# Where the halves of a modulation sum stand among the evictions of the block ahead of it

## Chip, cores and metric

The kernel runs on one core of one Trainium2 chip. A core has TensorE (PE, matmuls; its weight loads are shown as PEld), VectorE (DVE), ScalarE (ACT), GpSimd (POOL) and SyncE (SP, whose queue issues nearly all DMAs here). Each engine works off its own queue in order, and the engines meet at semaphores. The metric is the device time in microseconds, as the median of several runs.

## What is computed

The reference, cut to what matters (x is 64 x 64 x 512, cond is 64 x 256; all in fp32):

```python
q = relu(cond @ W3 + b3)                                  # 64 x 512
v = (64 * x + x.sum(axis=1, keepdims=True)) * q[:, None]  # the modulation
y = relu(v @ W2 + b2)
base   = y @ W_base + b_base
shared = (y @ A_s) @ B_s
gates  = softmax(y @ W_router + b_router)                 # 6 experts, the best 2 kept
routed = sum over e of ((y @ A_r[e]) * w[e]) @ B_r[e]
out = x + base + shared + routed
```

The sum over axis 1 is the modulation sum: for each of the 64 batches and each feature, a sum over 64 tokens.

## The kernel before

The 4096 tokens are worked on in four blocks k of 1024 tokens (16 batches). Features lie on the partitions in four chunks of 128, which are taken in the order `CHUNKS = (0, 2, 1, 3)`. A block has two stages.

The **first stage** makes y = relu(v @ W2 + b2). Block 0 has its own form, `first_mixed`, in which the first half of its tokens is computed directly, and the second half with sums of rows and of weights (a Strassen-like scheme with seven products; the products are made by `product`, L170). Blocks 1 to 3 use `first_inner`, the same scheme nested twice (L446).

Behind it PE computes **ph** (L779), the product of y with the low-rank matrices and the router. DVE makes the row sums **sy** of y (L263 to L266), and the **second stage**, `second`, begins: `gate` (L578 to L604, on DVE, with one exponential on ACT), then the products with W_base (L170, banks named ox, oy, oz, ow), copies on ACT that seed one bank from another (L629), the transposes of the gated low-rank values hw (L704), and the routed products (L641).

While a block is in these stages, the kernel prepares the *next* block. `prepare(k)` builds the list `behind` for block k. An entry of this list is a few steps, and `fill(n)`, called at fixed places between the current block's work, takes the next n entries off and issues them. The order is written out by hand: an engine's queue holds exactly what the calls issue, in their order. The steps are:

- `sums(c, half)` (L206 to L208, DVE): for chunk c and one half of the 16 batches, the reduction over the tokens (L207) and its product with q (L208); half 0 also makes 64 q (`nq`, L206) for all 16.
- `batch(c, b)` (L212, ACT): modulates one batch of one chunk in place, with `nq` as scale and the sum as bias.
- steps of weight sums (`also`, L137 to L140 and L161 to L164), and of row sums (L263 to L266, L315 to L318), on DVE.

The pairs are 32 entries with two batches each, eight for each chunk. Sums are put into chosen pairs, ahead of the batches: those of the second chunk (chunk 2) into pairs 4 and 5, those of the later ones into pairs 16, 19 and 20. Each of the first four `also` steps (L137 to L140) stands at the end of one of the first four pairs. Before all pairs stands one entry with both halves of the sum of the first chunk.

In `first_mixed` the calls are one `fill(1)` directly behind `prepare(1, ...)`, and then, for each of two rounds j:

```python
            product(py, 6, j, t2, s, start=j == 0)
            nc.vector.tensor_tensor(u, py, p1[:, j], ALU.add)        # L408
            product(pw, 5, j, t2, s, start=j == 0)
            nc.vector.tensor_tensor(r, pw, u, ALU.add)               # L410
            product(pz, 7, j, t2, s, start=j == 0)
            nc.vector.tensor_tensor(r, pz, r, ALU.add)               # L412
            relu(y, f2, 1, r, other)
            fill(1)
            product(pw, 3, j, t2, s, start=False)                    # r2: L416
            ...
            fill(1)
            product(pz, 4, j, t2, s, start=False)                    # r1: L420
            ...
            fill(1)
```

The second product into pw adds to the bank that L410 reads, so it waits for L410. Behind the second round follow ph on PE, sy on DVE, a fill of 8 entries (in block 0) or 4 (later blocks), and `second`.

Of the kernel before, what the change touches and what calls it, by code (L numbers as in the profile page):

```python
# [36 lines left out]
def adaln_ffn(ctx: ExitStack, tc: tile.TileContext, xa, x0, x1, head, w3, w2, wb, a, bcat, br, outT):  # L37
# [25 lines left out]
    def load_x(k):  # L63
        xs[k] = xpool.tile([P, NC, 2, TB], F32, tag="x", name=f"x_{k}")
        for c in CHUNKS:
            nc.sync.dma_start(xs[k][:, c].rearrange("p h t -> p (h t)"), x1[k, c])
# [126 lines left out]
    def modulate(k):  # L193


        vs[k] = v = xs[k]
        vsum = small.tile([P, NC, BB], F32, tag="vsum", name=f"vsum_{k}")
        nq = small.tile([P, NC, BB], F32, tag="nq", name=f"nq_{k}")

        def sums(c, half):  # L200

            bs = ts(half, BB // 2)
            xc = v[:, c].rearrange("p h (b n) -> p b h n", n=NH)[:, bs]
            q = q_sb[:, c, ts(k, BB)]
            if half == 0:
                nc.vector.tensor_scalar(nq[:, c], q, float(N), None, ALU.mult)  # L206
            nc.vector.tensor_reduce(vsum[:, c, bs], xc, AX.XY, ALU.add)  # L207
            nc.vector.tensor_tensor(vsum[:, c, bs], vsum[:, c, bs], q[:, bs], ALU.mult)  # L208

        def batch(c, b):  # L210
            x = v[:, c, :, ts(b, NH)]
            nc.scalar.activation(x, x, AF.Identity, bias=vsum[:, c, b : b + 1], scale=nq[:, c, b : b + 1])  # L212

        return ({c: [lambda c=c, n=n: sums(c, n) for n in range(2)] for c in CHUNKS},
                {c: [lambda c=c, b=b: batch(c, b) for b in range(BB)] for c in CHUNKS})
# [39 lines left out]
    def row_sums(a, name, cols=slice(0, TB)):  # L255

        all_s = mid.tile([P, 4, KH, TB], F32, tag=name, name=name)
        s = [all_s[:, i, :, cols] for i in range(4)]
        a11, a12, a21, a22 = a[:, :KH, 0, cols], a[:, KH:, 0, cols], a[:, :KH, 1, cols], a[:, KH:, 1, cols]

        def steps(c=slice(0, KH)):
            return [
                lambda: nc.vector.tensor_tensor(s[0][:, c], a21[:, c], a22[:, c], ALU.add),  # L263
                lambda: nc.vector.tensor_tensor(s[1][:, c], s[0][:, c], a11[:, c], ALU.subtract),
                lambda: nc.vector.tensor_tensor(s[2][:, c], a11[:, c], a21[:, c], ALU.subtract),
                lambda: nc.vector.tensor_tensor(s[3][:, c], a12[:, c], s[1][:, c], ALU.subtract),  # L266
            ]

        return {1: a11, 2: a12, 3: s[3], 4: a22, 5: s[0], 6: s[1], 7: s[2], "sums": all_s}, steps

    behind = []

    def fill(n):
        for _ in range(min(n, len(behind))):
            for step in behind.pop(0):
                step()

    def prepare(k, also=()):

        if k == NB:
            return
        sums, batches = modulate(k)
        ss[k], row_steps = row_sums(vs[k], "s")
        early, late = row_steps(slice(0, 1)), row_steps(slice(1, 2))
        c0, c1, c2, c3 = CHUNKS
        pairs = [batches[c][b : b + 2] for c in CHUNKS for b in range(0, BB, 2)]
        for places, steps in (((4, 5), sums[c1]), ((16, 16), sums[c2]), ((19, 20), sums[c3]),
                              ((25, 27, 29, 31), early)):  # L290
            for n, step in zip(places, steps):
                pairs[n].insert(0, step)
        for n, step in enumerate(also):
            pairs[n if n < 4 else 12 + n].append(step)
        behind.append(sums[c0])
        behind.extend(pairs)
        behind.extend([step] for step in late + prepare_inner(k))

# [43 lines left out]
    def first_mixed(y):  # L342
# [51 lines left out]
        for step in t2_steps + inner_steps[:4] + s_steps():  # L394
            step()
        prepare(1, tb_steps + inner_steps[4:])
        fill(1)
        pairs = temps(0)
# [25 lines left out]
    def first_inner(k, y):  # L424


        order = (1, 5, 6, 7, 2, 3, 4)
        prepare(k + 1)
        t_side, s_side = inner_t, inner[k]["s"]
        inner[k]["places"]()  # L430
# [87 lines left out]
        q(2, 1)  # L518
        for step in inner[k]["late"]:
            step()  # L520
        fill(1)
        for t in range(2, 7):
            open_banks(t)
            take_1(t - 2)
# [81 lines left out]
    def load_rows(k):  # L606

        res = {}
        for n, (f, h) in zip(pair_tags[2:3] + pair_tags[:2] + pair_tags[3:], ((1, 0), (1, 1), (0, 0), (0, 1))):
            res[f, h] = tmp.tile([P, KH, TB], F32, tag=n, name=f"x{n}_{k}")  # L610
            nc.sync.dma_start(
                res[f, h], x1[k, f * KH : (f + 1) * KH, :, ts(h, TB)].rearrange("c p t -> p c t")
            )
        return res
# [143 lines left out]
    for k in range(NB):  # L758
        y = mid.tile([P, NC, 2, TB], F32, tag="y", name=f"y_{k}")
        rest = None  # L760
        if k == 0:
            first_mixed(y)
        else:
            rest = first_inner(k, y)
        res = load_rows(k)
        if k == 0:
            load_x(3)

        ph = ps_h.tile([P, 2 * NS, P], F32, tag="ph", name=f"ph_{k}")
        groups = [(h, s) for h in range(2) for s in range(NS)]
        if not rest:
            groups.sort(key=lambda g: g[1] // KH)
        for n, (h, s) in enumerate(groups):
            if rest and n == 2:
                rest()
            for c in range(NC):
                nc.tensor.matmul(  # L779
                    ph[:, h * NS + s, :HC], y[:, c, h, ts(s, P)], a_sb[:, c, :],  # L780
                    start=(c == 0), stop=(c == NC - 1),
                )
        sys_[k], steps = row_sums(y, "sy")
        for step in steps():
            step()
        fill(4 if k else 8)
        second(k, y, ph, res)


# [48 lines left out]
```

## Time and profile before

| | us |
|---|---|
| median of 3 runs | 262.75 (262.47 to 262.76) |
| the profiled execution | 262.98 |
| its span | 261.2 |
| PE busy | 255.4 (98% of the span) |
| DVE busy | 193.9 (74%) |
| ACT busy | 136.6 (52%) |
| POOL busy | 38.7 (15%) |
| share of the chain that ended last: PE, DVE, ACT, DMA | 87%, 7%, 2%, 2% |

Block 0's stages lie in the span as follows: `first_mixed` to 35.2 us, ph from 35.2 to 42.5, the second stage to 74.2, where block 1's first product starts. Two stretches of it, from the table of windows (the columns are the length, then the busy time and number of instructions of PE, PEld, DVE, ACT and POOL, the granted clock of PE, the DMA share and GB/s):

```profile
27.24:29.08 1.84, 1.02 (x5) 0.57 (x4) 1.65 (x5) 0.00 (x0) 0.00 (x0) 1.00 0.95 376
29.08:35.23 6.15, 6.15 (x29) 5.42 (x30) 5.28 (x13) 4.42 (x12) 0.00 (x0) 1.00 0.30 119
```

In the first of them PE is busy for 1.02 of 1.84 us; in the second, all the time. A line of the timeline is: start, length, engine, line, operation, output and inputs with their shapes, number of instructions merged, and in brackets how long the engine had idled before it and what ended that. Matmuls of a timeline overlap, so that the start of a group is a better mark than its end.

### The profile page before, as it was taken

What the parts mean: (1) busy time and instruction counts of PE and PEld (TensorE: products, weight loads), DVE (VectorE), ACT (ScalarE), POOL (GpSimd) and SP (SyncE); (2) the same over time, 40 slices, a digit from 0 to 9 for tenths busy, and PEclk for the clock granted to TensorE, in tenths of its full rate; (3) what the DMA queues carried; (4) which work ended last, traced back from release to release, by engine and by line L of the source; (5) the groups of instructions that cost most, each with busy time, mean ns of one, the idle gap of its engine ahead of it and who ended that gap; (6) DMA issues with size and microseconds to landing.
All of it is one profiled execution on the core that took longest, in us unless ns stands there. A gap on an engine that the chain in (4) does not pass through costs nothing.

```text
span 261.2 us, 3176 instructions
## 1 busy us (share of the span) xinstructions
PE 255.4 (98%) x1004; PEld 164.6 (63%) x1004; DVE 193.9 (74%) x386; ACT 136.6 (52%) x373; POOL 38.7 (15%) x53
## 2 busy tenths in 40 slices
PE   7999899999999999999999999999999999999995
PEld 3755797454468889445458889644447889745452
DVE  2899987879968976967995894987895476872332
ACT  2299586588037897279106889349504428112000
POOL 1000000001008420002005640001000770000100
PEclk9999999999999999999999999999999999999999
DMA  7997719503320045000431025200332022400133
GB/s 167 382 337 285 282 32 375 235 3 111 130 80 0 4 148 174 0 3 0 164 117 41 0 80 160 86 0 3 120 120 80 0 74 92 160 0 3 72 141 109
DMA packets 14145, 28.54 MB, mean 109 GB/s; under 512 B 1472, under 2 KB 2496, under 8 KB 14128
## 3 DMA queue, kind: packets, MB, share of 16 engines
q1 hardware_dynamic: 13840, 28.21, 30.8%
q8 instruction: 8, 0.13, 0.2%
q10 hardware_dynamic: 288, 0.13, 0.2%
q14 instruction: 9, 0.07, 0.1%
HBM read 19.94 MB, written 8.39 MB: 108 GB/s over the span
## 4 chain that ended last, share of the span: by engine, by line
PE 87%; DVE 7%; ACT 2%; DMA 2%; issue 0%; SPq 0%; DVEq 0%
PE ia L446 13%; PE ph L779 11%; PE oz L170 11%; PE ox L170 11%; PE ib L446 10%; PE ow L170 9%; PE oy L170 5%; PE ow L641 5%; PE ox L641 3%; PE oz L641 3%; DMA w_sb<-in_w_dram 2%; DVE vsum L228 1%; PE pt L704 1%; PE last L650 1%; ACT y L340 1%; PE yw L170 1%
## 5 line engine op out<-in xcount | busy, mean ns | idle before, releaser
L212 ACT ACTIVATE x<-x,vsum,nq 128x64 f32<-128x64 f32 x192 | 67.6, 431 | 7.0 <-DVE vsum L208 7.0
L779 PE MATMUL ph<-a_sb,y 128*128 128x118 f32 x256 | 30.5, 276 | 0.3 <-ACT y L340 0.3
L779 PEld LDWEIGHTS ph<-a_sb,y 128*128 128x128 f32 x256 | 30.0, 192 | 1.2 <-ACT y L340 0.7
L437 DVE TENSOR_TENSOR u<-ib,u 128x256 f32<-128x256 f32 x42 | 16.4, 418 | 18.5 <-PE ib L446 18.3
L452 ACT COPY ib<-ia 128x256 f32<-128x256 f32 x21 | 7.6, 360 | 42.3 <-PE ia L446 42.3
L170 PE MATMUL ox<-y,wb_sb 128*128 128x512 f32 x64 | 29.5, 593 | 0.0
L708 POOL TENSOR_TENSOR hwd<-hwT 112x512 f32<-112x512 f32 x4 | 5.8, 1451 | 137.6 <-ACT hwT L706 137.6
L170 PEld LDWEIGHTS ox<-y,wb_sb 128*128 128x128 f32 x64 | 11.9, 190 | 13.4 <-issue 13.2
L437 DVE TENSOR_TENSOR u<-ia,u 128x256 f32<-128x256 f32 (+1 forms) x36 | 16.1, 461 | 2.9 <-ACT u L484 1.6
L340 ACT ACTIVATE y<-u,head_sb 128x256 f32<-128x256 f32 (+1 forms) x30 | 15.8, 584 | 4.0 <-DVE u L412 4.0
L446 PE MATMUL ib<-inner_s,inner_t 128*128 128x256 f32 x60 | 17.8, 384 | 0.0
L637 DVE SCALAR_TENSOR_TENSOR xu<-oz,head_sb,xu 128x512 f32<-128x512 f32 x16 | 12.0, 749 | 7.2 <-PE oz L170 4.8
L207 DVE TENSOR_REDUCE vsum<-x 128x8 f32<-128x512 f32 x24 | 16.2, 675 | 0.0
L170 PE MATMUL oz<-sy,tb 128*128 128x512 f32 x32 | 15.2, 599 | 0.0
L170 PE MATMUL oz<-y,tb 128*128 128x512 f32 x32 | 15.1, 592 | 0.0
L170 PE MATMUL oy<-sy,tb 128*128 128x512 f32 x32 | 15.0, 592 | 0.0
L354 PE MATMUL py<-v,w_sb 128*128 128x512 f32 (+1 forms) x40 | 14.4, 510 | 0.6 <-DMA w_sb<-in_w_dram 0.6
L170 PE MATMUL ow<-sy,wb_sb 128*128 128x512 f32 x28 | 13.2, 592 | 0.0
L170 PE MATMUL ow<-sy,tb 128*128 128x512 f32 x28 | 13.2, 592 | 0.0
L455 ACT COPY ib<-ib 128x256 f32<-128x256 f32 x21 | 7.6, 363 | 9.9 <-PE ib L446 9.9
L446 PEld LDWEIGHTS ib<-inner_s,inner_t 128*128 128x128 f32 x60 | 11.2, 190 | 2.2 <-ACT ib L455 0.8
L250 ACT ACTIVATE v<-x,vsum,nq 128x64 f32<-128x64 f32 x32 | 11.0, 428 | 1.9 <-DVE vsum L248 1.9
(173 smaller groups left out, 462.2 us busy)
## 6 DMA issues: line engine op xcount, KB each, us to landing
xu<-in_x_dram SPq DMA_DIRECT2D x16, 512.0 KB, 4.2
out_dram<-xu SPq DMA_DIRECT2D x30, 256.0 KB, 2.0
x<-in_x_dram SPq DMA_DIRECT2D x12, 512.0 KB, 7.8
x<-in_x_dram SPq DMA_DIRECT2D x7, 256.0 KB, 5.7
w_sb<-in_w_dram SPq DMA_DIRECT2D x4, 256.0 KB, 5.7
wb_sb<-in_wb_dram SPq DMA_DIRECT2D x4, 256.0 KB, 5.1
w_sb<-in_w_dram SPq DMA_DIRECT2D x1, 384.0 KB, 5.5
out_dram<-xu SPq DMA_DIRECT2D x2, 192.0 KB, 1.9
```

The costliest lines, as they stand in the source:

```text
L170: nc.tensor.matmul(ps, w[i][:, c, ts(j, P)], s[i][:, c, :], start=start and c == 0, stop=c == KH - 1, skip_group_check=True,)
L207: nc.vector.tensor_reduce(vsum[:, c, bs], xc, AX.XY, ALU.add)
L212: nc.scalar.activation(x, x, AF.Identity, bias=vsum[:, c, b : b + 1], scale=nq[:, c, b : b + 1])
L250: nc.scalar.activation(v[:, c, :, ts(b, NH)], batches_of(c, b, b + 1)[:, :, 0], AF.Identity, bias=vsum[:, c, b : b + 1], scale=nq[:, c, b ...
L340: nc.scalar.activation(y[:, f, h, cols], src, AF.Relu, bias=b2_sb[:, f : f + 1])
L354: nc.tensor.matmul(p[:, :, lo * NH : hi * NH], w2_sb[:, c, ts(f, P)], v[:, c, :, lo * NH : hi * NH], start=(c == 0 and lo == 0), stop=(c = ...
L437: add = lambda o, a, b: nc.vector.tensor_tensor(o, a, b, ALU.add)
L446: nc.tensor.matmul(bank[b, t][:, cols], t_side(o, n), s_side(o, n), start=n == 1, stop=True, skip_group_check=True,)
L452: nc.scalar.copy(bank["b", t][:, lo], bank["a", t][:, lo])
L637: nc.vector.scalar_tensor_tensor(t, ps[name, j], bb_sb[:, f : f + 1], t, ALU.add, ALU.add)
L641: nc.tensor.matmul(ps[name, j], bcat_sb[:, ts(f, P)], hw, start=False, stop=True, skip_group_check=True)
L779: nc.tensor.matmul(ph[:, h * NS + s, :HC], y[:, c, h, ts(s, P)], a_sb[:, c, :], start=(c == 0), stop=(c == NC - 1),)
```

## The change

```diff
@@ prepare
-        for places, steps in (((4, 5), sums[c1]), ((16, 16), sums[c2]), ((19, 20), sums[c3]),
+        for places, steps in (((4, 4 if k == 1 else 5), sums[c1]), ((16, 16), sums[c2]), ((19, 20), sums[c3]),
                               ((25, 27, 29, 31), early)):
...
-        behind.append(sums[c0])
+        behind.extend([step] for step in sums[c0])
         behind.extend(pairs)
@@ first_inner
         for step in inner[k]["late"]:
             step()
-        fill(1)
+        fill(2)
@@ the loop over blocks
-        fill(4 if k else 8)
+        fill(4 if k else 9)
         second(k, y, ph, res)
```

The one entry with both halves of the first chunk's sum becomes two entries with one half each. In `first_mixed` the `fill(1)` behind `prepare(1, ...)` thus issues half 0 alone, half 1 comes with the first fill of the first round (behind L412), and each pair one fill later than before. In `first_inner` the first fill takes two entries in place of one, so that both halves still come together there. The fill ahead of block 0's second stage takes 9 entries in place of 8, so that the same entries are left for the second stage. For block 1's preparation (k == 1) both halves of chunk 2's sum now stand in pair 4 (half 1 first, since each is inserted at the front); pair 4 is what the last fill of the second round issues.

## The prediction

> **What bounds the kernel now.** I read the busy table first: TensorE (PE) is busy 98% of the 261.2 us span, and in the chain that ended last it holds 87%. So almost any saving must be a place where PE stands still. I therefore went to the list of waits and looked for PE as the waiting engine, then to the timeline of PE and VectorE (DVE) around the one entry that lies in the code that is changed. From the list of waits (engine, line, what was waited for: us in total, times, longest):
>
> ```profile
> PEld yw L170 <- DVE u L410: 1.2, 1, 1.2
> PE yw L170 <- DVE u L410: 0.8, 1, 0.8
> DVE lg L578 <- PE ph L779: 0.8, 1, 0.8
> ```
>
> PE waits once, in block 0, for the eviction at L410. The timeline of PE there (start, us, what):
>
> ```profile
> 26.37 1.03 PE L170 MATMUL yw<-s,t 128*128 128x256 f32 x4
> 27.24 1.03 PE L170 MATMUL yz<-s,t 128*128 128x256 f32 x4
> 29.08 1.13 PE L170 MATMUL yw<-s,w_sb 128*128 128x256 f32 x4 [0.82 <-DVE u L410]
> 30.05 1.03 PE L170 MATMUL yz<-v,t 128*128 128x256 f32 x4
> ```
>
> A group of four normally starts 0.86 us after the one before (26.37 to 27.24). Between yz and yw it is 1.84, so the stall is **0.98 us** from start to start. What DVE did meanwhile:
>
> ```profile
> 26.49 0.68 DVE L207 TENSOR_REDUCE vsum<-x 128x8 f32<-128x512 f32 x1
> 27.20 0.17 DVE L208 TENSOR_TENSOR vsum<-vsum,q_sb 128x8 f32<-128x8 f32 x1
> 27.28 0.68 DVE L207 TENSOR_REDUCE vsum<-x 128x8 f32<-128x512 f32 x1
> 27.99 0.17 DVE L208 TENSOR_TENSOR vsum<-vsum,q_sb 128x8 f32<-128x8 f32 x1
> 28.08 0.42 DVE L408 TENSOR_TENSOR u<-yy,p 128x256 f32<-128x256 f32 x1
> 28.60 0.42 DVE L410 TENSOR_TENSOR u<-yw,u 128x256 f32<-128x256 f32 x1
> 29.13 0.42 DVE L412 TENSOR_TENSOR u<-yz,u 128x256 f32<-128x256 f32 x1
> ```
>
> The two pairs L207/L208 are the two halves of the modulation sum of chunk 0 for the next block. Both stand ahead of L408 and L410, and L408's input yy had been ready for 1.5 us (yy ended at 26.53). The chain that ended last goes through exactly these rows: the DVE sums of s, the two halves, L408, L410, then yw, and from there PE nearly alone to the end.
>
> **What is removed from the path.** The second half (27.28 to 28.08, start to start **0.80 us**) now stands behind L412. L408 starts at 27.28. L410 waits for L408's result, and the two start 0.52 apart, so L410 runs from 27.80 to 28.22; its other input, yw, ended at 27.40. PE was released 0.06 after L410 ended (29.02 to 29.08), so yw starts at 28.28. Sum: 29.08 - 28.28 = **0.80 us** earlier. PE alone could have started at 28.10 (27.24 + 0.86), so 0.18 of the stall stays, and 0.98 is the most that this place can yield.
>
> One rule asks for a different size. The Trainium skill, "VectorE: DVE Perf Modes", section "The DRAIN you can't avoid", has each DVE operation followed by a flush of about its duration less 266 ns in which the next one doesn't start. Read as time behind the operation, a half would free 0.68 + 0.41 + 0.17 = 1.26 us, and PE's own pace would then cut the gain to 0.98. The rows say otherwise: L208 starts 0.71 behind an L207 of 0.68, and L408 starts 0.09 behind an L208 of 0.17. I take 0.80. The same skill's "TensorE: Matmul & The Clock Gate", first part, has PE's clock halved after an idle window of some 3.4 us; a stall of 0.98 is far under it, and the granted clock is 1.00 in the windows around it, so no clock bonus is added to the 0.80.
>
> **What is added behind L412.** L412 then runs at 28.33 (yz, which it needs, ends at 28.27), and its release of the next product yz is in time. The half follows and with it everything in DVE's queue: L416, L137, L420, L138, then the second round's L408, L410. Three things ask for these:
> - PE's second-round yw needs yw's bank read by L416. L416 starts at 29.64 (28.33 + 0.51 + 0.80) and ends at 30.06; the product starts at 31.77 - 0.80 = 30.97. Slack 0.9. Likewise L420, ending near 31.0, against 31.84. Both cost nothing.
> - The second L410 must let PE's second yw<-s,w_sb start, which stood at 33.50 and now wants 32.70. From L412 to the second L408 DVE took 2.99 (29.13 to 32.12). One fill step (L139, 0.60 start to start) drops behind, the half (0.80) comes in: 3.19. So L408 starts at 31.52, and L410 at 32.04, just when its product is done (32.80 - 0.80 = 32.00). It ends at 32.46, releases at 32.52, and 0.18 is left. **This is the thinnest cover of the change.** If DVE is later by more than 0.18, PE waits for the rest, one for one.
> - ScalarE's (ACT's) relu evictions wait for L416 and L420. ph (64 rows, started at 35.23) needs the columns that they write only behind its first 32 rows, 3.6 us after its start: before, the last of them ended at 36.81, against 38.8. Nothing.
>
> **What moves ahead of the gate.** The pairs of batches slip by one place. In the second round L139 and L140 fill the two gaps, and both halves of chunk 2's sum (0.80 each and an L206 of 0.08) come behind the last L420, which makes the last eviction earlier: L412 32.90, L139 33.24, L416 33.84, L140 34.18, L420 34.78 to 35.20, instead of an end at 36.27. The row sums sy begin 3.28 + 0.60 = 3.88 behind the second L412, at 36.78 (before: 36.98), and end 4.75 later, at 41.53. The gate's first row L578 waits for ph, whose end moves from 42.53 to 41.73. So the 0.84 of idle time of DVE there shrinks to about 0.2, but stays: the gate starts 0.80 earlier too. If that cover were gone, DVE would be late at the gate only; its result hw (47.89) is asked for by PE at 56.11, so nothing follows. ACT: the last eviction starts near 35.24; behind it 20 batches instead of 18, at 0.337 each (6.06/18), from 35.65 to 42.39, and the exponential wants ACT at 43.28 - 0.80 = 42.48. It fits, just. Its queue holds the seed copies next, and the first of them wants 43.55. SP: its four row loads wait for the last eviction and go out about 1.05 earlier, and the four loads of x behind them too; nothing waits on them before 48.33. POOL's queue is passed by nothing.
>
> **Behind the gate** the number of queued steps is the same as before, and so is each engine's order in blocks 1 to 3: there both halves still stand in one place, since two entries are taken where one was. Both queue ends behind the gate are released by PE: DVE idles 0.44 for ACT's copy of a PE result, ACT idles 11.02 before block 1. So the 0.80 is a plain shift of all that follows; the only non-PE pieces in the later chain (ACT evictions near 94 and 155, and a DVE row at 258) are themselves behind PE.
>
> **Sum.** The profiled execution took 262.98 (span 261.2, 1.78 around it): 262.98 - 0.80 = 262.18. It stood 0.23 above the median of the three runs, 262.75, so against that median: **261.95 us**. 0.2%, about what a measurement of this kernel can tell from no change, is 0.53 us; the three runs lie within 0.29.
>
> **Rivals.**
> - *The wait comes back in the second round.* For it: only 0.18 of cover at the second L410, and L137 carries two waits for transfers, which is where the 0.51 behind L412 came from. Against it: the weights were issued by 13.5 and landed within 5.6. If DVE is 0.55 late there, 0.37 is handed back: gain 0.43, **262.3**.
> - *The shift is swallowed later.* For it: block 1 has DVE finishing inner_s at 75.4 while PE is already in that block, so PE there is close to being DVE's. Against it: DVE's busy stretch before it is released by ACT batches that follow PE's transposes, so it shifts too. If two thirds go there: **262.5**.
> - *Slower: ACT's longer run of batches.* Twenty batches stand between the last eviction and the gate's exponential and seed copies. The copy of y is asked for by PE at 45.0, and can start at 43.55 and end at 44.12; ACT must be 1.7 us behind my sum before PE waits, and 2.5 before the gain is gone. If the batches took 0.49 each in place of 0.337 (20 x 0.15 = 3.0 us), the end is **263.2**. Batches of this kind ran at 0.337 in that very stretch, so I hold it unlikely.
> - *That the change doesn't do what it says* I see no room for: the order of DVE's instructions moves as told.
>
> **How the numbers follow.** 0.80 gained (between 0.65 and 0.98): 81%. Second round: 9%. Swallowed: 6%. Slower: 4%. The likeliest gives 261.95. Its gain bounds (0.98 and 0.65) give 261.77 and 262.10; with the spread of the runs (0.15 each way) 261.6 to 262.25, and up to 262.35 it takes in most of the second-round case. Faster by over 0.2% (under 262.22): nearly all of the first case and a fifth of the second, 80%. Within 0.2%: 16%. Slower: 4%.
>
> **What would show it.** PE's yw at about 28.3 with a wait of about 0.1; the second yw<-s,w_sb without one; ph at 34.4; L578 still waiting for ph, by 0.1 to 0.3; block 1's first ia near 73.4 instead of 74.17; granted clock 1.00. Wrong would be: PE waiting for DVE in front of the second yw, the first yw earlier by less than 0.7, or later blocks whose distance from ph has changed.

## Result

| | before | changed |
|---|---|---|
| median of 11 runs each, us | 262.65 | 261.70 (261.42 to 262.31) |
| ratio, 95% interval | | 0.9966 (0.9949 to 0.9982) |
| profiled execution, its span, us | 262.98, 261.2 | 261.56, 259.8 |

The kernel became faster by 0.95 us in these runs, 0.36%; 261.95 had been forecast. The whole interval lies under 1, and its upper end (0.18%) just within what was called no change.

PE's timeline of the changed kernel, over the same products as before:

```profile
24.77 1.10 PE L170 MATMUL yy<-s,t 128*128 128x256 f32 x4
25.71 1.03 PE L170 MATMUL yw<-s,t 128*128 128x256 f32 x4
26.58 1.03 PE L170 MATMUL yz<-s,t 128*128 128x256 f32 x4
27.63 1.13 PE L170 MATMUL yw<-s,w_sb 128*128 128x256 f32 x4
28.59 1.03 PE L170 MATMUL yz<-v,t 128*128 128x256 f32 x4
...
32.05 1.03 PE L170 MATMUL yw<-s,w_sb 128*128 128x256 f32 x4
32.91 1.03 PE L170 MATMUL yz<-v,t 128*128 128x256 f32 x4
33.77 7.30 PE L779 MATMUL ph<-a_sb,y 128*128 128x118 f32 x64
```

From yz to yw it is now 1.05 us instead of 1.84. No wait is noted in brackets, but 0.19 over the pace of 0.86 is left: yw starts 0.06 behind the end of L410, as before. The second round runs at 0.86 from group to group. DVE's timeline of the same kernel shows the half in its new place, and what is left of DVE's idle time ahead of the gate:

```profile
26.54 0.17 DVE L208 TENSOR_TENSOR vsum<-vsum,q_sb 128x8 f32<-128x8 f32 x1
26.62 0.42 DVE L408 TENSOR_TENSOR u<-yy,p 128x256 f32<-128x256 f32 x1
27.15 0.42 DVE L410 TENSOR_TENSOR u<-yw,u 128x256 f32<-128x256 f32 x1
27.68 0.43 DVE L412 TENSOR_TENSOR u<-yz,u 128x256 f32<-128x256 f32 x1
28.02 0.68 DVE L207 TENSOR_REDUCE vsum<-x 128x8 f32<-128x512 f32 x1
...
30.68 0.41 DVE L408 TENSOR_TENSOR u<-yy,p 128x256 f32<-128x256 f32 x1
31.39 0.42 DVE L410 TENSOR_TENSOR u<-yw,u 128x256 f32<-128x256 f32 x1 [0.29 <-PE yw L170]
...
41.11 0.21 DVE L578 TENSOR_TENSOR lg<-ph,br_sb 128x48 f32<-128x48 f32 x1 [0.23 <-PE ph L779]
```

The two profiled spans differ by 1.4 us, more than the medians. So the span has to be cut into pieces that can be compared: to the first yy, from there to the start of ph, to block 1's first ia, and to the end. Each start is read from PE's timeline.

| us | to first yy | yy to ph | ph to first ia | ia to the end |
|---|---|---|---|---|
| before | 25.43 | 9.80 | 38.94 | 187.0 |
| changed | 24.77 | 9.00 | 38.95 | 187.1 |

All that the change does is in the second piece: **0.80 us**. The first piece is 0.66 shorter here, but lies ahead of anything that was moved; the last section shows where its scatter comes from. The pieces behind ph are equal to 0.1 us, so nothing was handed back.

In the chain that ended last, the DVE work between yy and the second yw is gone; the chain now stays on PE there (the chain of the changed kernel in order of time; columns are start, length, what):

```profile
25.88 0.86 PE yw L170 x4
26.74 0.86 PE yz L170 x4
27.63 1.13 PE yw L170 x4
```

Ahead of yy the chain says less about the change. In the kernel before it went mainly over DVE from 9.84 on, in this profile of the changed kernel over PE; but in the first run below, which has the same split, it goes over DVE again, up to L264 at 24.76.

### The profile page after: what moved, and what is told of

The parts are those of the page before. It is cut to its first block, busy times and chain, and to the rows that moved or that the text cites. A ratio compares the mean times of both kernels' runs of the same rounds, so it can differ in the third digit from the quotient of the medians.

```text
span 259.8 us, 3177 instructions
## 1 busy us (share of the span) xinstructions
PE 254.8 (98%) x1004; PEld 164.5 (63%) x1004; DVE 193.9 (75%) x386; ACT 136.5 (53%) x373; POOL 38.7 (15%) x53
## 4 chain that ended last, share of the span: by engine, by line
PE 94%; ACT 2%; DMA 2%; SPq 0%; issue 0%; DVE 0%
PE ia L446 13%; PE ph L779 11%; PE oz L170 11%; PE ox L170 11%; PE ib L446 10%; PE ow L170 9%; PE py L354 5%; PE oy L170 5%; PE ow L641 5%; PE oz L641 3%; PE ox L641 3%; DMA w_sb<-in_w_dram 2%; PE yw L170 1%; PE pt L704 1%; PE last L650 1%; PE yz L170 1%
## 5 line engine op out<-in xcount | busy, mean ns | idle before, releaser
L207 DVE TENSOR_REDUCE vsum<-x 128x8 f32<-128x512 f32 x24 | 16.2, 676 | 0.0
```

## Experiments

The piece from yy to ph is the measure in all of them. It hardly depends on when the first transfers land: in all eleven profiles yy starts 0.83 or 0.84 us behind the start of DVE's L264 (the second of block 0's own row sums s), so that PE and DVE enter the piece at the same distance in time.

**The split alone.** The change without its edit of chunk 2's places:

```diff
-        for places, steps in (((4, 4 if k == 1 else 5), sums[c1]), ...
+        for places, steps in (((4, 5), sums[c1]), ...
```

> Chunk 0's sum is split over two entries as in the change, chunk 2's halves stay in pairs 4 and 5, so one of them now stands between sy and the gate. Theory (the half ahead of the evictions of round one was the stall): the whole gain stays; from the first yy to the start of ph 9.0 us (before 9.80), time 0.8 us under the kernel before. DVE reaches L578 at the same point, since sy starts 0.8 us earlier and the half follows it. Rival (clearing the stretch ahead of the gate, or the earlier last eviction, brought it): no gain, 9.8 us from yy to ph, or a gain that shows only behind ph.

yy to ph 9.00, median 261.68 against 262.48 of the kernel before beside it, ratio 0.9967 (0.9955 to 0.9979). The split of chunk 0's sum carries the whole gain. The two ends of the piece in PE's timeline of this run:

```profile
24.89 1.10 PE L170 MATMUL yy<-s,t 128*128 128x256 f32 x4 [0.24 <-DVE s L264]
33.89 7.30 PE L779 MATMUL ph<-a_sb,y 128*128 128x118 f32 x64
```

What the new places of chunk 2 do is seen on ACT alone: without them the gate's exponential starts 8.53 behind ph (42.42), with them 8.11. The first seed copy starts 9.12 behind ph in both, so this is cover and no time.

**The places alone.** The kernel before with only that edit:

```diff
-        for places, steps in (((4, 5), sums[c1]), ...
+        for places, steps in (((4, 4 if k == 1 else 5), sums[c1]), ...
```

> Only chunk 2's halves are moved (both into pair 4); both halves of chunk 0 stay in one entry ahead of L408. Theory: the stall stays, 9.8 us from yy to ph, time as before within 0.2 us; the last eviction is 0.8 us later, and PE doesn't wait for it. Rival: 0.3 to 0.8 us faster than before.

yy to ph 9.79, median 262.58 against 262.48, ratio 1.0001 (0.9992 to 1.001). The wait stands where it stood (PE's timeline of this run):

```profile
26.78 1.03 PE L170 MATMUL yz<-s,t 128*128 128x256 f32 x4
28.62 1.13 PE L170 MATMUL yw<-s,w_sb 128*128 128x256 f32 x4 [0.82 <-DVE u L410]
29.59 1.03 PE L170 MATMUL yz<-v,t 128*128 128x256 f32 x4
```

So moving chunk 2's halves together is worth nothing by itself. Nor is keeping the stretch between sy and the gate free of sums: in the run before this one a half stood there, and ph to ia was 38.94 as well.

**A half more in round one.** How thin is the cover of the second L410? The changed kernel with one half (0.80 us) moved ahead of the second L408:

```diff
-        for places, steps in (((4, 4 if k == 1 else 5), sums[c1]), ...
+        for places, steps in (((4, 1 if k == 1 else 5), sums[c1]), ...
```

> The changed kernel with half 1 of chunk 2's sum (0.80 us of DVE) put three pairs earlier, into the last fill of round one, ahead of the second L408. Theory: the cover at the second L410 is 0.2 us and then PE pays one for one: a stall of about 0.6 us ahead of the second yw<-s,w_sb, 9.6 us from yy to ph, and the time 0.6 us over the changed kernel, 0.2 us under the one before. Rival (PE has more slack there, since it is busy without a gap): no stall, time as the changed kernel.

yy to ph 9.53, which is 0.53 over the changed kernel; median 262.17, against 261.68 of the split alone in the same set (ratios to the kernel before: 0.9989, 0.9981 to 0.9997, and 0.9967, 0.9955 to 0.9979). PE's and DVE's timelines of this run:

```profile
31.25 1.03 PE L170 MATMUL yz<-s,t 128*128 128x256 f32 x4
32.55 1.13 PE L170 MATMUL yw<-s,w_sb 128*128 128x256 f32 x4 [0.27 <-DVE u L410]
33.52 1.03 PE L170 MATMUL yz<-v,t 128*128 128x256 f32 x4
```

```profile
31.55 0.42 DVE L408 TENSOR_TENSOR u<-yy,p 128x256 f32<-128x256 f32 x1
32.07 0.42 DVE L410 TENSOR_TENSOR u<-yw,u 128x256 f32<-128x256 f32 x1
```

The step from yz to yw is 1.30, 0.44 over the pace. The 0.80 divides up as follows. In the changed kernel DVE would have been ready for L410 0.52 behind the second L408, at 31.20, and began at 31.39 for want of yw: 0.19 of it was idle time. L410 then ended at 31.81 and could have released PE 0.06 later, at 31.87; PE's yw started at 32.05 at its own pace, so PE still had 0.18. The remaining 0.43 is paid one for one (0.44 measured), and the next step is 0.97 instead of 0.86, another 0.11. Together that is 0.54 or 0.55, where 0.53 was measured. The wait that is noted in brackets, 0.27, shows only half of the loss: it is counted from the end of the matmuls in front, which are 0.17 longer than their pace.

**Sums ahead of the gate.** The changed kernel with 1.68 us of DVE work between sy and the gate:

```diff
-        for places, steps in (..., ((16, 16), sums[c2]), ...
+        for places, steps in (..., ((13, 13) if k == 1 else (16, 16), sums[c2]), ...
```

> The changed kernel with both halves of chunk 1's sum (1.68 us of DVE with their nq) moved from pair 16 to pair 13, so that they stand between sy and the gate. As predicted on record (only the gate is late, nothing asks for hw before 56 us): the gate is 1.45 us late (1.68 less the idle 0.23), the time is that of the changed kernel within 0.2 us. Rival: the exponential stands ahead of the seed copies in ACT's queue; it then ends near 43.6 us, the first copy of y starts 0.75 us or so late and ends 1.2 us late or more, and PE waits 0.2 to 0.5 us for it at oy; 0.2 to 0.5 us over the changed kernel.

yy to ph 8.99, ph to ia 38.95, median 261.88 (ratio 0.997, 0.995 to 0.999): as the changed kernel within the scatter. DVE and ACT of this run (ph starts at 34.45), then PE:

```profile
43.14 0.20 DVE L578 TENSOR_TENSOR lg<-ph,br_sb 128x48 f32<-128x48 f32 x1
```

```profile
43.85 0.24 ACT L585 ACTIVATE g<-lg 128x48 f32<-128x48 f32 x1 [1.20 <-DVE lg L583]
44.00 0.58 ACT L629 COPY oy<-ox 128x512 f32<-128x512 f32 x1
```

```profile
45.03 1.88 PE L170 MATMUL oy<-sy,tb 128*128 128x512 f32 x4
```

L578 starts 8.69 behind ph's start; in the changed kernel it was 7.34 (41.11 - 33.77). The gate is 1.35 late. 1.45 had been expected, from the 0.23 of idle time noted in brackets; counted from start to start the room is larger, since L266 is followed by L578 at 1.45 in the changed kernel and by the next sum at 1.14 here, which leaves 0.31. The late gate does hold up the seed copy, as the rival had it: it starts 9.55 behind ph instead of 9.12. But it ends at 44.58, and PE asks for it at 45.03. The cover at the gate is real, and with 1.35 us used, 0.45 of it is left on the way over ACT.

**Both halves behind.** What is left of the stall, and can it be had? Half 0 goes behind L412, half 1 behind L416; three weight-sum steps go one pair later and the fourth behind the gate, to free DVE ahead of the second L410 (changes against the changed kernel):

```diff
-        for places, steps in (((4, 4 if k == 1 else 5), sums[c1]), ...
+        for places, steps in (((3, 3) if k == 1 else (4, 5), sums[c1]), ...
-            pairs[n if n < 4 else 12 + n].append(step)
+            pairs[n + 1 if n < 3 else 14 if n == 3 else 12 + n].append(step)
         prepare(1, tb_steps + inner_steps[4:])
-        fill(1)
-        fill(4 if k else 9)
+        fill(4 if k else 10)
```

With it ran the changed kernel once more.

> The changed kernel once more, beside the run below on one chip: 0.8 us under the kernel before in the median; 9.0 us from the first yy to ph. The part of its first profile that lay ahead of yy (0.66 us earlier than before) should not be a property of it: theory, that part is scatter of the first transfers, and the start of yy lies between 24.7 and 25.5 us whatever the kernel; rival, it is always earlier than in the kernel before.

> Both halves of chunk 0's sum behind the evictions of round one (half 0 behind L412, half 1 behind L416), the weight-sum steps L137 to L139 one pair later and L140 behind the gate, chunk 2's halves in pair 3. Theory: L408 then starts as soon as yy is done, L410 ends 0.15 us before PE wants the bank, the rest of the stall (0.19 us from start to start) goes too; 8.8 us from yy to ph, time 0.2 us under the changed kernel, 1.0 us under the one before. The gate is some 0.4 us late, and ACT's queue has room for that. Rival: the second round, which has 0.2 us of cover, is now late and gives back 0.2 us or more: as the changed kernel or slower.

The changed kernel: yy to ph 9.00, median 261.66 against 262.51. Its yy started at 25.49, not at 24.77, so the early start of its first profile was no property of it. The other: yy to ph **8.71**, median 261.51, ratio 0.9961 (0.9949 to 0.9974). PE's timeline of the latter:

```profile
27.11 1.03 PE L170 MATMUL yz<-s,t 128*128 128x256 f32 x4
27.97 1.03 PE L170 MATMUL yw<-s,w_sb 128*128 128x256 f32 x4
28.84 1.03 PE L170 MATMUL yz<-v,t 128*128 128x256 f32 x4
```

Nothing of the stall is left: 0.86 and 0.87. It yields 0.29, not the 0.19 that was expected, since the step behind the wait becomes shorter too (0.96 to 0.87). The gate starts 0.27 later behind ph than in the changed kernel, at no cost: ph to ia is 38.93.

**Both halves behind, weight sums where they were.** As above, but with the line `pairs[n if n < 4 else 12 + n].append(step)` of the changed kernel. Beside it ran the version above and the changed kernel.

> The kernel with both halves of chunk 0's sum behind the evictions of round one, but with the weight-sum steps L137 to L140 left in pairs 0 to 3, so that one of them (0.60 us of DVE) stands ahead of the second L408. Theory (a stall ends only if DVE's load ahead of the second L410 falls too): the first stall is gone, L410 of the second round ends 0.16 us too late, and the restart of PE costs 0.10 more: 8.97 us from yy to ph, the time of the changed kernel. Rival (the 0.29 us came from the first round alone): 8.71 us, and 0.3 us under the changed kernel.

> The kernel with both halves behind and the weight sums later, once more: 8.71 us from yy to ph; 1.0 to 1.1 us under the kernel before in the median, 0.2 to 0.3 under the changed kernel.

> The changed kernel beside the two others on one chip: 9.00 us from yy to ph, 0.8 to 0.9 us under the kernel before in the median.

| | yy to ph | median of the runs | ratio to before, 95% |
|---|---|---|---|
| weight sums stay | 8.97 | 261.69 | 0.9969 (0.9951 to 0.9986) |
| both behind, again | 8.71 | 261.36 | 0.9967 (0.9949 to 0.9985) |
| changed, again | 9.00 | 261.60 | 0.9969 (0.9952 to 0.9986) |

With the weight sums left in place the wait goes from round one to round two, to within 0.03 us (PE's timeline of that run):

```profile
31.24 1.03 PE L170 MATMUL yz<-s,t 128*128 128x256 f32 x4
32.26 1.13 PE L170 MATMUL yw<-s,w_sb 128*128 128x256 f32 x4
33.23 1.03 PE L170 MATMUL yz<-v,t 128*128 128x256 f32 x4
```

1.02 and 0.97: nearly all that the first round gains, the second loses. The version with both halves behind is 0.29 us shorter from yy to ph than the changed one in both pairs of profiles, and 0.15 and 0.24 us in the medians; the intervals of the ratios overlap widely, so in total time it is not shown to beat the changed kernel.

## Why the prediction was right

- **The half ahead of L408 is the stall.** Right, in place and size. Counted from the start of yz, L408 was put at 0.04, L410 at 0.56 and yw at 1.04; measured 0.04, 0.57 and 1.05. The gain is 0.80 in the trace, and the two separate edits show that all of it comes from the split.
- **"0.98 is the most that this place can yield."** Too small. The version without a stall yields 9.80 - 8.71 = 1.09. The sum counted the stall from start to start, and left out that the group after a wait needs 0.96 or 0.97 us to the next one, not 0.86. This didn't touch the forecast, because a short wait remained in the changed kernel and this 0.10 with it.
- **"PE waits once, in block 0."** There is a second, shorter wait for DVE, which the list of waits doesn't show. In the kernel before, the product behind a set of eight yx starts 1.73 us after it (18.29 to 20.02), but from the second such set to yy it is 1.98:

```profile
23.45 1.89 PE L361 MATMUL yx<-v,w_sb 128*128 128x256 f32 x8
24.59 0.69 DVE L264 TENSOR_TENSOR s<-s,v 128x512 f32<-128x512 f32 x1
25.43 1.10 PE L170 MATMUL yy<-s,t 128*128 128x256 f32 x4
```

  So PE lost 0.25 there, ahead of everything that was moved; over the eleven profiles it is 0.04 to 0.51, and in three of them the row of yy names L264 as what it waited for. The change doesn't touch this wait, so the forecast didn't need it, but what stands ahead of L264 in DVE's queue is a further place to look.
- **Between the flush behind each DVE operation and the rows of the trace**, the rows were right: 0.80, and not the 0.98 that the longer reading gave. That reading had also left out a part of the section in the Trainium skill ("VectorE: DVE Perf Modes", "The DRAIN you can't avoid"): it calls the flush a gap from start to start, and says that an operation that is not held starts earlier. Here L207 starts 0.34 behind an L412 of 0.43, before the latter's end. No clock effect came in between yy and the end; the granted clock was 1.00 in both kernels' profiles.
- **The second round.** It was put at a start of L410 just when its input is ready, with 0.18 of cover for PE behind that. PE's 0.18 was right. DVE had another 0.19, since L207 starts 0.34 behind L412 and not 0.51. The 0.51 had been laid to the two waits for transfers at L137; in the changed kernel L137 starts 0.34 behind L416 with the same waits. What made it 0.51 before stays open.
- **The gate.** sy was put 9.54 behind yz's start (36.78 - 27.24) and stands at 9.55. DVE's idle time there is 0.23, where about 0.2 was forecast. ACT "fits, just": the 20 batches take 6.73, and the exponential starts 0.08 behind the end of L583 where it was 0.03 before. That a late gate costs nothing held with 1.35 us of lateness; but its first consumer is not hw at 56 us, as the prediction had it, but the seed copies behind the exponential, with 0.45 us left.
- **A plain shift of all that follows.** Right: ph to ia and ia to the end are equal in all profiles to 0.1 us. Of the rivals, the wait in the second round is real but needs more DVE work ahead of it than the change puts there; nothing was swallowed, and ACT's longer run of batches made the exponential of the changed kernel late by less than 0.1.
- **The total.** 261.70 measured, 261.95 forecast. The forecast took its gain from 262.75, the median of three runs; more runs of the kernel before gave 262.65, 262.48, 262.51 and 262.54. Against the runs beside it the changed kernel gained 0.95, 0.85 and 0.94, and the split alone 0.80. So 0.80 is at the lower end of these, and the trace shows no second source. That the total came out 0.25 under the forecast is thus scatter of the medians and of the start, as far as the traces show.

## What to carry to other kernels

When an engine that is busy 98% of the time waits once, look at what stands in its releaser's queue ahead of the releasing instruction, and move what nobody is waiting for behind it; then add up the releaser's load again up to the next place where the busy engine asks for something, because the wait turns up there as soon as the idle time in between is used. Count a stall from start to start, and add the slower step that follows it. Compare two profiles piece by piece between events of the bound engine; spans as a whole carry the scatter of the first transfers.

## What the runs showed of the hardware

- **A matmul group after a wait is slower once.** Its step to the next group was 0.96 to 0.97 us in all ten places of the eleven profiles where a yw had waited for L410, by 0.16 to 0.98 us, against 0.86 to 0.87 without a wait. In the timeline of the weight loads (PEld) of the kernel before, yw's first load starts together with its first matmul, at 29.08, where that of the next group starts 0.22 ahead (29.83 and 30.05). That the load that couldn't run ahead is the cause is argued, not tested.
- **A DVE operation that reads the result of the one ahead of it starts later.** L410 starts 0.52 to 0.53 behind L408, whose result it reads, while L207 starts 0.34 behind L412, and L137 0.34 behind L416, with operations of the same length (0.42 or 0.43 us) in front. One row doesn't fit: in the kernel before L137 starts 0.51 behind L412, which it doesn't read.
- **The start scatters more than the change is worth, and the traces show where.** yy began between 24.66 and 26.66 us over eleven profiles. Ahead of it the first products of py, which in most profiles wait for the transfer of w_sb, began between 5.80 and 6.83. From there to yy it is 18.62 to 18.66 us in ten profiles, once the wait for L264 is taken off. So of the 0.66 between the two kernels' first profiles, 0.45 is a later py (6.55 and 6.10) and 0.21 the longer wait for L264 (0.25 and 0.04).
- **In the eleventh profile PE ran at half its pace at the start.** It is the second of the version with both halves behind, whose profiled execution took 263.12 us, 1.76 over the median:

```profile
6.21 3.74 PE L354 MATMUL py<-v,w_sb 128*128 128x256 f32 x8 [0.27 <-DMA w_sb<-in_w_dram]
```

  These eight matmuls took 1.96 to 2.00 us in the others. They start 0.43 us apart, against 0.22 in the kernel before. In this trace the record of the granted clock, with 1.00, begins only at 9.82 us, about where they end; in the other ten it begins between 3.49 and 6.10, ahead of py. No trace has a value ahead of that record, so the 1.00 that a window shows there is not measured. A clock of one half would fit the pace, and 0.50 is the only other value on record (behind the last products, in ten of the traces). Why full speed came late here is not shown.
